# A decoder layer on one core: four key products of the context attention placed among the second projections, and rope's swap of halves done by copies on ACT

## The chip, the cores and the metric

The kernel runs on one core of a Trainium2 chip. The time is that of the device, in microseconds (us), for the whole program; the number that counts is the median of several runs. A profile of one execution stands beside it, taken by the hardware profiler.

The core's engines work side by side, each through its own queue and strictly in the order of that queue: PE (TensorE: matmuls), DVE (VectorE: elementwise work), ACT (ScalarE: activation functions, copies with a conversion), POOL (GpSimd: here, sums and maxima over the partitions) and SP (SyncE: here, it issues the DMAs). PE writes into PSUM, which is divided into eight banks; everything else lies in SBUF.

## The reference: what is computed

One decoder layer in fp32 on 8 batches of 100 tokens, D = 1024, with a context of 722 tokens for each batch:

```python
def _L0_xattn_ref(x, h_ctx_kv, ...):
    q = (x @ wq).reshape(B, L, NUM_HEADS, HEAD_DIM)          # 16 heads of 128
    k = (x @ wk).reshape(B, L, NUM_KV_HEADS, HEAD_DIM)       # 4 of 128
    v = (x @ wv).reshape(B, L, NUM_KV_HEADS, HEAD_DIM)
    q = rms_norm(q, q_norm_w)
    k = rms_norm(k, k_norm_w)
    k_ctx = (h_ctx_kv @ wk_ctx).reshape(B, T, NUM_KV_HEADS, HEAD_DIM)
    v_ctx = (h_ctx_kv @ wv_ctx).reshape(B, T, NUM_KV_HEADS, HEAD_DIM)
    k_ctx = rms_norm(k_ctx, k_norm_w)
    q = q * cos + rotate_half(q) * sin
    k = k * cos + rotate_half(k) * sin
    k_full = jnp.concatenate([k_ctx, k], axis=1)
    ...                                                       # causal softmax attention
    return out.reshape(B, L, NUM_HEADS * HEAD_DIM) @ wo

x = _layernorm(x + _L0_attn_ref(x, ...))      # retention, 8 heads
x = _layernorm(x + _L0_xattn_ref(x, context, ...))
x = _layernorm(x + _L0_ffn_ref(x, ...))       # silu(gate) * up, then down
```

The products that the change moves are `h_ctx_kv @ wk_ctx` for two of the four kv heads of batch 0. The swap of halves is `rotate_half`, in the queries and keys of the tokens (not of the context).

## The kernel before, in words

Every activation is kept transposed, features on the 128 partitions and tokens along the free axis. The 800 tokens are worked on in two halves of N = 400 (four batches each). So that fp32 accuracy comes out of the matmul's fp32r format, each operand is held as two parts, hi and lo: `split` makes hi by a cast on ACT (L69) and lo by a subtraction on DVE (L70). Each product is then three matmuls (`mm3`: L88 hi·hi, L89 hi·lo, L90 lo·hi), and a projection of 1024 features to 128 (`proj`) is 8 x 3 = 24 matmuls into one bank of PSUM. Banks come in three groups (L52): three of tag "a", four of "s", one of "v".

A weight comes in through `load_w`: a DMA of 512 KB into one of three buffers `wst`, then a split into one of four buffers `w`. The context weights were split earlier and lie in DRAM as `wcd`; `load_ws` brings one in as a DMA of 1 MB straight into a `w` buffer.

The stages follow each other: retention attention (l1), its output projection with LayerNorm (`out_proj`, half 0 and then half 1; its results are the split activations `z1`), the second projections (pool "l2"), the context attention (pool "cx"), the second output projection with LayerNorm, the feed-forward part. The order inside each engine's queue is not written out by hand: the framework's scheduler simulates the program with its own durations (L998) and orders each queue by that, so instructions of neighbouring stages are mixed at the seams. An order once fixed is kept by each engine.

Second projections, l2 (L570–594). For each of four kv heads there are four query heads (i = 0 to 3), one key (i = 4) and one value (i = 5), for both halves: 48 projections of `z1`, whose banks alternate between "a" and "s". A value is transposed, split and stored. Each of the 40 queries and keys goes through this:

- ACT squares the bank (L585), POOL sums the squares over the partitions (`all_red`, L127, into one of two buffers `ss`);
- `rope` (L130–140) multiplies the bank by the cosines (L136, whole) and by the sines with the halves of the partitions swapped (L137 and L138, 64 partitions each), all three on DVE reading PSUM, and adds the two results (L139, both in SBUF). After L138 the bank is free;
- `inv_root` (L112–123) makes the inverse root of the sum: Ln, Exp and Square on ACT (L115, L118, L120), two multiplies on DVE (L121 reads `ss` for the last time, L122);
- DVE multiplies the two (L590), `split2` divides the result into `d` (L69 on ACT, L70 on DVE), and SP stores it to DRAM (`qd`, `kd`).

Context attention, cx (L600 on). For each batch b, the context comes in through eight DMAs of 360 KB (`cs`, in the same three `wst` buffers; L609) and eight splits into four tiles `big`. Then for each kv head: two products for the keys (`proj(wk, ...)`, 362 and 360 columns), each followed by a square on ACT (L629), a sum over the partitions on POOL (L630), and the scaled keys as hi (ACT, L631) and lo (DVE, L632) in `kall`; two products for the values, which are transposed; scores; softmax; and the product with the values.

The tail of the LayerNorm of half 1 (`norm_late`, L298–309, and `scaled`, L264–269) stands right before the projections of half 1: a matmul gives the mean's last part (`delta`), ACT squares it (L304), DVE subtracts it from eight tiles `y` (L308) and from the variance (L305), `inv_root` follows, and for each of the eight tiles DVE scales `y` (L266), ACT casts it to hi and DVE subtracts for lo (L69, L70: these write `z`, that is `z1` of half 1).

Of the kernel before, what the change touches and what calls it, by code (L numbers as in the profile page):

```python
# [8 lines left out]
F32 = mybir.dt.float32  # L9
FR = mybir.dt.float32r  # L10
# [6 lines left out]
P = 128  # L17
# [24 lines left out]
def decoder_layer(ctx, tc, xT, cT, w1, wo1, w2, wo2, wc, w3, wd, gw, qw, kw, trig, dec, mask, out):  # L42
    nc = tc.nc

    def sbuf(name, bufs, side=None):
        return tc.tile_pool(name=name, bufs=bufs, side=side, reuse_waits="tile")
# [11 lines left out]
    def f32(ap):  # L58
        return ap.bitcast(F32)

    def bt(ap):
        return ap.rearrange("p (b t) -> p b t", b=NB)

    def split(dst, src):

        split2(dst[:, 0], dst[:, 1], src)
# [5 lines left out]
    def load_w(src, w=None, parts=1):  # L72
        st = wp.tile([P, KT * P], F32, tag="wst", name="wst", bufs=3)
        if w is None:
            w = wp.tile([P, 2, KT * P], FR, tag="w", name="w", bufs=4)
        for i in range(parts):
            c = slice(i * KT * P // parts, (i + 1) * KT * P // parts)
            nc.sync.dma_start(out=st[:, c], in_=src[:, c])
            split(w[:, :, c], st[:, c])
        return w  # L80

    def load_ws(i):
        w = wp.tile([P, 2, KT * P], FR, tag="w", name="w", bufs=4)
        nc.sync.dma_start(out=f32(w), in_=f32(wcd[i]))
        return w
# [16 lines left out]
    def proj(w, z, n=N, tag="a"):  # L102
        acc = bank(tag)[:, :n]
        for k in range(KT):
            t = z[k // QT]
            mmw(acc, w, k, t[:, 0, k % QT, :n], t[:, 1, k % QT, :n], k == 0, k == KT - 1)
        return acc
# [19 lines left out]
        nc.gpsimd.partition_all_reduce(y, x, P, op)  # L127
        return y

    def rope(pool, acc, cosw, sinw, tag="t1"):  # L130

        t1 = pool.tile([P, N], F32, tag=tag, name=tag)
        t2 = pool.tile([P, N], F32, tag="t2", name="t2")
        a = bt(acc)
        h = P // 2
        nc.vector.tensor_tensor(bt(t1), a, cosw[:, None, :].to_broadcast([P, NB, T]), ALU.mult)  # L136
        nc.vector.tensor_tensor(bt(t2[0:h]), a[h:P], sinw[h:P, None, :].to_broadcast([h, NB, T]), ALU.mult)  # L137
        nc.vector.tensor_tensor(bt(t2[h:P]), a[0:h], sinw[0:h, None, :].to_broadcast([h, NB, T]), ALU.mult)  # L138
        nc.vector.tensor_tensor(t1, t1, t2, ALU.add)  # L139
        return t1  # L140

    def tokens_first(pool, acc, copied=True):
# [23 lines left out]
    def big(shape):  # L166
        return bp.tile(shape, FR, tag="big", name="big")
# [29 lines left out]
    def load_constants(p, trg):  # L197
        dcy = p.tile([T, NH1, T], F32, name="dcy", bufs=1)
        nc.sync.dma_start(out=dcy, in_=dec)
        nc.sync.dma_start(out=msk, in_=mask)  # L200
        nc.sync.dma_start(out=wts[:, 0:2], in_=gw)
        nc.sync.dma_start(out=wts[:, 2:3], in_=qw)
        nc.sync.dma_start(out=wts[:, 3:4], in_=kw)

        nc.vector.tensor_scalar(gws, wts[:, 0:2], -8.0, None, ALU.mult)
        nc.vector.tensor_scalar(kws, wts[:, 3:4], -0.5 * math.sqrt(P), None, ALU.mult)
        nc.vector.tensor_scalar(tq, trg[:, 2:4], wts[:, 2:3], None, ALU.mult)
        nc.vector.tensor_scalar(tk, trg[:, 2:4], wts[:, 3:4], None, ALU.mult)
        return dcy


# [187 lines left out]
    with sbuf("l1", 2) as p:  # L399
# [37 lines left out]

        r4 = []

        def rope1(acc, cosw, sinw, tag):  # L440

            t1 = p.tile([P, N], F32, tag=tag, name=tag)
            t2 = p.tile([P, N], F32, tag="t2", name="t2")
            h = P // 2
            nc.scalar.copy(t2[0:h], acc[h:P])
            nc.scalar.copy(t2[h:P], acc[0:h])
            nc.vector.tensor_tensor(bt(t1), bt(acc), cosw[:, None, :].to_broadcast([P, NB, T]), ALU.mult)
            nc.vector.tensor_tensor(bt(t2), bt(t2), sinw[:, None, :].to_broadcast([P, NB, T]), ALU.mult)
            nc.vector.tensor_tensor(t1, t1, t2, ALU.subtract)
            return t1  # L450


        HB = ((0, 0), (1, 1), (0, 1), (1, 0))
        qk, v, oo, ss = {}, {}, {}, {}

        def of_qk(half, i, acc):
            qk[half, i] = rope1(acc, trg[:, 2 * i], trg[:, 2 * i + 1], f"qk{i}")

        def of_v(half, blk, acc, copied):
            tr = tokens_first(p, acc, copied)  # L460
# [106 lines left out]

    kapool = sbuf("ka", 2, "right")
    ka = kapool.__enter__()
    with sbuf("l2", 2) as p:  # L570
        for kv in range(NKV):
            for i0, i1 in ((0, 4), (4, 6)) if kv == 0 else ((0, 2), (2, 4), (4, 6)):
                ws = [load_w(w2[kv, i]) for i in range(i0, i1)]
                for half in range(2):
                    bs = slice(half * NB, (half + 1) * NB)
                    for i in range(i0, i1):
                        acc = proj(ws[i - i0], z1[half], tag=acc_tag())
                        if i == 5:
                            tr = tokens_first(p, acc).rearrange("p (b d) -> p b d", b=NB)
                            vs = p.tile([T, NB, 2, P], FR, tag="vs", name="vs", bufs=1)  # L580
                            split2(vs[:, :, 0], vs[:, :, 1], tr)
                            nc.sync.dma_start(out=f32(vd[kv, :, bs]), in_=f32(vs))
                            continue
                        sq = p.tile([P, N], F32, tag="sq", name="sq")
                        nc.scalar.activation(sq, acc, AF.Square)  # L585
                        ss = all_red(p, sq, "ss")
                        tb = tq if i < 4 else tk
                        t = rope(p, acc, tb[:, 0], tb[:, 1])
                        r = inv_root(p, ss, eps_k)
                        nc.vector.scalar_tensor_tensor(  # L590
                            t, t, -0.5 if i < 4 else -0.5 * math.sqrt(P), r, ALU.mult, ALU.mult)
                        d = p.tile([P, NB, 2, T], FR, tag="d", name="d", bufs=3)
                        split2(d[:, :, 0], d[:, :, 1], bt(t))
                        nc.sync.dma_start(out=f32(qd[kv, i, :, bs] if i < 4 else kd[kv, :, bs]), in_=f32(d))
# [4 lines left out]
    y2p = y2pool.__enter__()  # L599
    with sbuf("cx", 2) as p, sbuf("c1", 1) as p1:  # L600
        for b in range(B):
            cz = []
            for hf in range(2):
                n = SN[hf]
                z = [big([P, 2, QT, SH]) for _ in range(2)]
                for k in range(0, KT, 2):
                    cs = wp.tile([P, KT * P], F32, tag="wst", name="cs", bufs=3)
                    cs = cs[:, :2 * n].rearrange("p (k n) -> p k n", k=2)
                    nc.sync.dma_start(out=cs, in_=cT[b, :, k:k + 2, hf * SH:hf * SH + n])  # L609
                    split(z[k // QT][:, :, k % QT:k % QT + 2, :n], cs)  # L610
                cz.append(z)
            for kv in range(NKV):

                kall = ka.tile([P, 2, SC + T], FR, tag="kall", name="kall")
                nc.sync.dma_start(out=f32(kall[:, :, SC:]), in_=f32(kd[kv, :, b]))
                vall = p.tile([P, NC, 2, P], FR, tag="vall", name="vall")
                nc.sync.dma_start(out=f32(vall[C5:P, 5]), in_=f32(vd[kv, 0:P - C5, b]))
# [1 line left out]
                q = p.tile([P, 4, 2, T], FR, tag="q", name="q")  # L619
                nc.sync.dma_start(out=f32(q).rearrange("p h l t -> p h (l t)"),  # L620
                                  in_=f32(qd[kv, :, :, b]).rearrange("h p l t -> p h (l t)"))
                wk, wv = load_ws(2 * kv), load_ws(2 * kv + 1)
                sq = ka.tile([P, SC], F32, tag="ksq", name="ksq", bufs=1)
                ss = ka.tile([P, 6 * P], F32, tag="kss", name="kss", bufs=1)
                nc.gpsimd.memset(ss[:, SC:], 1.0)
                for hf in range(2):
                    n, at = SN[hf], slice(hf * SH, hf * SH + SN[hf])
                    acc = proj(wk, cz[hf], n)
                    nc.scalar.activation(sq[:, at], acc, AF.Square)  # L629
                    nc.gpsimd.partition_all_reduce(ss[:, at], sq[:, at], P, RED.add)  # L630
                    nc.scalar.activation(kall[:, 0, at], acc, AF.Copy, scale=kws)  # L631
                    nc.vector.scalar_tensor_tensor(kall[:, 1, at], acc, kws, f32(kall[:, 0, at]), ALU.mult, ALU.subtract)  # L632
                vt = p.tile([P, SC], F32, bufs=1, tag="cvt", name="cvt")
                for hf in range(2):
                    copy = nc.scalar.copy if hf == 0 else nc.vector.tensor_copy
                    copy(vt[:, hf * SH:hf * SH + SN[hf]], proj(wv, cz[hf], SN[hf]))
                for c0, c1, rows in ((0, 3, P), (3, 5, P), (5, 6, C5)):
                    tr = bank("s")
                    for c in range(c0, c1):
# [1 line left out]
                    src = tr[0:rows, 0:(c1 - c0) * P].rearrange("p (c d) -> p c d", d=P)  # L641
                    split2(vall[0:rows, c0:c1, 0], vall[0:rows, c0:c1, 1], src)

                row = dr.tile([6, P], F32, tag="row", name="row", bufs=2)
                nc.sync.dma_start(out=row.rearrange("c p -> (c p)")[None, :], in_=ss[0:1])
                rr = p.tile([P, 6], F32, tag="rr", name="rr")
                with nc.allow_non_contiguous_dma("a row turned into a column"):
                    nc.sync.dma_start(out=rr, in_=row.rearrange("c p -> p c"))
# [354 lines left out]
```

## Time and profile before

| what | value |
|---|---|
| runs, median (lowest to highest) | 2560.26 us (2559.32 to 2564.6) |
| profiled execution: own time | 2563.27 us |
| profiled execution: span | 2561.5 us |
| mean granted clock of PE | 0.993 |
| matmuls of l2 | from 572.4 to 829.9 us |
| rope in l2 on DVE | from 604.1 to 845.1 us |
| matmuls of one 128x400 product, start to start | 0.182 us |
| all-reduces, L127 writing `ss`: number, mean | 56, 2787 ns |

A busy time of an engine is the sum of its instructions' durations, where overlapping ones count once. "Idle before, releaser" is the time that an engine stood still ahead of an instruction, and the instruction that ended it. L-numbers are lines of the kernel before; a helper's line (L69, L70, L127) occurs in several stages, so its groups are told apart by the names of the tiles.

### The profile page before, as it was taken

What the parts mean: (1) busy time and instruction counts of PE and PEld (TensorE: products, weight loads), DVE (VectorE), ACT (ScalarE), POOL (GpSimd) and SP (SyncE); (2) the same over time, 40 slices, a digit from 0 to 9 for tenths busy, and PEclk for the clock granted to TensorE, in tenths of its full rate; (3) what the DMA queues carried; (4) which work ended last, traced back from release to release, by engine and by line L of the source; (5) the groups of instructions that cost most, each with busy time, mean ns of one, the idle gap of its engine ahead of it and who ended that gap; (6) DMA issues with size and microseconds to landing.
All of it is one profiled execution on the core that took longest, in us unless ns stands there. A gap on an engine that the chain in (4) does not pass through costs nothing.

```text
span 2561.5 us, 37457 instructions
## 1 busy us (share of the span) xinstructions
PE 2504.4 (98%) x14186; PEld 2464.7 (96%) x14186; DVE 2018.0 (79%) x3350; ACT 1294.3 (51%) x2310; POOL 468.8 (18%) x230
## 2 busy tenths in 40 slices
PE   8999999999988999999999999999999999999997
PEld 8999999998988999999999999999999999999996
DVE  6778876568999788898988988777865865865885
ACT  6676766335554455565656655444432432432451
POOL 0100011004444343433443443100000000000000
PEclk9999999999999999999999999999999999999999
DMA  7333445763335655454554455474411211211221
GB/s 236 108 125 120 147 142 207 247 227 114 135 131 181 200 176 165 144 177 147 160 174 152 154 183 176 149 259 131 153 50 66 83 50 65 84 50 65 68 74 52
DMA packets 165939, 353.91 MB, mean 138 GB/s; under 512 B 45531, under 2 KB 108379, under 8 KB 156543
## 3 DMA queue, kind: packets, MB, share of 16 engines
q1 hardware_dynamic: 164606, 347.33, 40.3%
q0 software_dynamic: 1152, 4.19, 1.0%
q8 instruction: 111, 1.82, 0.3%
q14 instruction: 70, 0.57, 0.1%
HBM read 283.09 MB, written 68.39 MB: 137 GB/s over the span
## 4 chain that ended last, share of the span: by engine, by line
PE 85%; DVE 9%; issue 2%; DMA 2%; ACT 1%; SPq 0%; DVEq 0%; ACTq 0%
PE a L88 16%; PE a L90 16%; PE a L89 16%; PE s L88 9%; PE s L89 9%; PE s L90 9%; PE v L88 3%; PE v L90 2%; PE v L89 2%; PE s L480 1%; DVE w L70 1%; DVE r L121 1%; DMA cs<-in_cT 1%; PE s L640 1%; DVE t L590 1%
## 5 line engine op out<-in xcount | busy, mean ns | idle before, releaser
L88 PE MATMUL a<-big,w 128*128 128x400 f32 (+2 forms) x1796 | 605.7, 338 | 7.3 <-ACT big L69 6.6
L89 PE MATMUL a<-big,w 128*128 128x400 f32 (+2 forms) x1796 | 605.2, 337 | 0.1
L90 PE MATMUL a<-big,w 128*128 128x400 f32 (+2 forms) x1796 | 603.8, 337 | 0.0
L69 ACT CAST w<-wst 128x1024 fp32r<-128x1024 f32 (+2 forms) x292 | 251.4, 864 | 271.2 <-PE a L90 120.0
L70 DVE TENSOR_TENSOR w<-wst,w 128x1024 fp32r<-128x1024 f32 (+2 forms) x292 | 294.2, 1010 | 107.3 <-ACT w L69 106.3
L88 PEld LDWEIGHTS a<-big,w 128*128 128x128 f32 x1796 | 338.2, 188 | 8.1 <-ACT big L69 6.6
L89 PEld LDWEIGHTS a<-big,w 128*128 128x128 f32 x1796 | 338.8, 189 | 1.6 <-DVE big L70 1.0
L90 PEld LDWEIGHTS a<-big,w 128*128 128x128 f32 x1796 | 339.0, 189 | 0.8 <-DVE w L70 0.2
L127 POOL PARTITION_ALL_REDUCE ss<-sq x56 | 155.6, 2787 | 358.3 <-DVE z L70 162.2
L88 PE MATMUL s<-big,w 128*128 128x400 f32 x596 | 207.9, 349 | 1.9 <-ACT big L69 1.9
L89 PE MATMUL s<-big,w 128*128 128x400 f32 x596 | 207.2, 348 | 2.0 <-DVE big L70 2.0
L90 PE MATMUL s<-big,w 128*128 128x400 f32 x596 | 206.4, 347 | 0.0
L630 POOL PARTITION_ALL_REDUCE kss<-ksq x64 | 167.9, 2624 | 142.2 <-ACT ksq L629 141.7
L69 ACT CAST w<-as 128x512 fp32r<-128x512 f32 x90 | 55.9, 621 | 213.2 <-PE a L90 180.8
L676 ACT ACTIVATE s<-s,rk 128x400 f32<-128x400 f32 x160 | 88.1, 591 | 93.7 <-DVE sm L698 60.6
L827 DVE TENSOR_TENSOR s<-s 128x400 f32<-128x400 f32 x183 | 102.7, 571 | 25.1 <-ACT s L823 19.3
L127 POOL PARTITION_ALL_REDUCE mb<-sm x32 | 83.3, 2602 | 200.9 <-DVE sm L698 200.9
L88 PEld LDWEIGHTS s<-big,w 128*128 128x128 f32 x596 | 112.7, 189 | 4.0 <-ACT big L69 3.1
L695 ACT ACTIVATE s<-s 128x800 f32<-128x800 f32 (+1 forms) x128 | 95.0, 749 | 42.2 <-DVE s L689 39.3
L89 PEld LDWEIGHTS s<-big,w 128*128 128x128 f32 x596 | 112.7, 189 | 3.4 <-DVE big L70 2.5
L90 PEld LDWEIGHTS s<-big,w 128*128 128x128 f32 x596 | 113.3, 190 | 0.0
L70 DVE TENSOR_TENSOR pl<-s,ph 128x800 fp32r<-128x800 f32 (+1 forms) x128 | 108.4, 851 | 2.1 <-ACT ph L69 1.5
(311 smaller groups left out, 6196.2 us busy)
## 6 DMA issues: line engine op xcount, KB each, us to landing
wst<-in_w SPq DMA_DIRECT2D x137, 512.0 KB
w<-wcd SPq DMA_DIRECT2D x64, 1024.0 KB
wst<-in_wo SPq DMA_DIRECT2D x64, 512.0 KB
wst<-in_wd SPq DMA_DIRECT2D x32, 512.0 KB
big<-o1d SPq DMA_DIRECT2D x16, 800.0 KB
qd<-d SPq DMA_DIRECT2D x32, 400.0 KB
q<-qd SPq DMA_DIRECT2D x32, 400.0 KB
o2d<-oh SPq DMA_DIRECT2D x32, 400.0 KB
```

The source lines that it names most:

```text
L69: nc.scalar.copy(hi, src)
L70: nc.vector.tensor_tensor(lo, src, f32(hi), ALU.subtract)
L88: nc.tensor.matmul(acc, lh, rh, start=start, stop=False, skip_group_check=chain)
L89: nc.tensor.matmul(acc, lh, rl, start=False, stop=False, skip_group_check=chain)
L90: nc.tensor.matmul(acc, ll, rh, start=False, stop=stop, skip_group_check=chain)
L121: nc.vector.scalar_tensor_tensor(q, ss, eps, q, ALU.add, ALU.mult)
L127: nc.gpsimd.partition_all_reduce(y, x, P, op)
L480: nc.tensor.matmul(bt(o)[:, b], vv[:, b * P:(b + 1) * P], pf[:, b], start=True, stop=True)
L630: nc.gpsimd.partition_all_reduce(ss[:, at], sq[:, at], P, RED.add)
L676: nc.scalar.activation(sc, sp, AF.Copy, scale=rk[:, c:c + 1])
L695: nc.scalar.activation(e, e, AF.Exp)
L827: nc.vector.tensor_tensor(t, x, y, op)
```

## The change

Three things are altered.

1. `rope` takes the form that the retention stage had under the name `rope1`: ACT copies the two halves of the bank, swapped, into `t2`; DVE multiplies the bank by the cosines and `t2` by the sines (this one reads SBUF alone), and adds. The two halves of the sine tables of queries and keys (`tq`, `tk`) are swapped once at the start, by six small copies. `rope1` is gone, and the retention stage calls `rope` with a subtraction.
2. The loads and splits of a batch's context become a function, `load_context`. That of batch 0 is called within l2, before the weights of kv 0's key and value (i0 = 4); in the order that the scheduler makes of it, its eight DMAs follow those of the weights of the first four projections on SP, and its splits stand among the tail of the LayerNorm of half 1. The other batches' are where they were.
3. The keys of the context become `context_keys`, with a `step` for each of the two parts. For batch 0, the keys of kv 0 and kv 1 are made within l2, one part ahead of each of four groups of projections. Their `kall` and their row of sums are kept in the list `early` until the context attention takes them. The values' `cvt` moves to the pool "ka".

```diff
-    def rope(pool, acc, cosw, sinw, tag="t1"):
+    def rope(pool, acc, cosw, sinw, tag="t1", op=ALU.add):
         t1 = pool.tile([P, N], F32, tag=tag, name=tag)
         t2 = pool.tile([P, N], F32, tag="t2", name="t2")
-        a = bt(acc)
         h = P // 2
-        nc.vector.tensor_tensor(bt(t1), a, cosw[:, None, :].to_broadcast([P, NB, T]), ALU.mult)
-        nc.vector.tensor_tensor(bt(t2[0:h]), a[h:P], sinw[h:P, None, :].to_broadcast([h, NB, T]), ALU.mult)
-        nc.vector.tensor_tensor(bt(t2[h:P]), a[0:h], sinw[0:h, None, :].to_broadcast([h, NB, T]), ALU.mult)
-        nc.vector.tensor_tensor(t1, t1, t2, ALU.add)
+        nc.scalar.copy(t2[0:h], acc[h:P])
+        nc.scalar.copy(t2[h:P], acc[0:h])
+        nc.vector.tensor_tensor(bt(t1), bt(acc), cosw[:, None, :].to_broadcast([P, NB, T]), ALU.mult)
+        nc.vector.tensor_tensor(bt(t2), bt(t2), sinw[:, None, :].to_broadcast([P, NB, T]), ALU.mult)
+        nc.vector.tensor_tensor(t1, t1, t2, op)
...
+        for t in (tq, tk):
+            sw = p.tile([P, T], F32, tag="vt", name="sw", bufs=1)
+            nc.vector.tensor_copy(sw, t[:, 1])
+            nc.vector.tensor_copy(t[0:P // 2, 1], sw[P // 2:P])
+            nc.vector.tensor_copy(t[P // 2:P, 1], sw[0:P // 2])
...
+    def load_context(b):
+        cz.clear()
+        for hf in range(2):
+            n = SN[hf]
+            z = [big([P, 2, QT, SH]) for _ in range(2)]
+            for k in range(0, KT, 2):
+                cs = wp.tile([P, KT * P], F32, tag="wst", name="cs", bufs=3)
+                cs = cs[:, :2 * n].rearrange("p (k n) -> p k n", k=2)
+                nc.sync.dma_start(out=cs, in_=cT[b, :, k:k + 2, hf * SH:hf * SH + n])
+                split(z[k // QT][:, :, k % QT:k % QT + 2, :n], cs)
+            cz.append(z)
+
+    def context_keys(kv):
+        kall = ka.tile([P, 2, SC + T], FR, tag="kall", name="kall")
+        wk = load_ws(2 * kv)
+        sq = ka.tile([P, SC], F32, tag="ksq", name="ksq", bufs=1)
+        ss = ka.tile([P, 6 * P], F32, tag="kss", name="kss", bufs=1)
+        row = dr.tile([6, P], F32, tag="row", name="row", bufs=2)
+        nc.gpsimd.memset(ss[:, SC:], 1.0)
+        def step(hf):
+            n, at = SN[hf], slice(hf * SH, hf * SH + SN[hf])
+            acc = proj(wk, cz[hf], n)
+            nc.scalar.activation(sq[:, at], acc, AF.Square)
+            nc.gpsimd.partition_all_reduce(ss[:, at], sq[:, at], P, RED.add)
+            nc.scalar.activation(kall[:, 0, at], acc, AF.Copy, scale=kws)
+            nc.vector.scalar_tensor_tensor(kall[:, 1, at], acc, kws, f32(kall[:, 0, at]), ALU.mult, ALU.subtract)
+            if hf:
+                nc.sync.dma_start(out=row.rearrange("c p -> (c p)")[None, :], in_=ss[0:1])
+        return step, (kall, row)
...
     with sbuf("l2", 2) as p:
         for kv in range(NKV):
             for i0, i1 in ((0, 4), (4, 6)) if kv == 0 else ((0, 2), (2, 4), (4, 6)):
+                if (kv, i0) == (0, 4):
+                    load_context(0)
                 ws = [load_w(w2[kv, i]) for i in range(i0, i1)]
+                if (kv, i0) in ((1, 2), (2, 2)):
+                    step, kept = context_keys(kv - 1)
+                    early.append(kept)
+                if (kv, i0) in ((1, 2), (2, 0), (2, 2), (3, 0)):
+                    step(i0 == 0)
...
-            cz = []
...
+            if b > 0:
+                load_context(b)
             for kv in range(NKV):
-
-                kall = ka.tile([P, 2, SC + T], FR, tag="kall", name="kall")
+                if early:
+                    kall, row = early.pop(0)
+                else:
+                    step, (kall, row) = context_keys(kv)
+                    step(0)
+                    step(1)
```

More of the change, by code (lines that the diff above doesn't have):

```diff
@@ L438, in decoder_layer @@
         r4 = []
[L440 to L450, printed above, removed]
         HB = ((0, 0), (1, 1), (0, 1), (1, 0))
@@ L456, in of_qk @@
         def of_qk(half, i, acc):
-            qk[half, i] = rope1(acc, trg[:, 2 * i], trg[:, 2 * i + 1], f"qk{i}")
+            qk[half, i] = rope(p, acc, trg[:, 2 * i], trg[:, 2 * i + 1], f"qk{i}", ALU.subtract)
         def of_v(half, blk, acc, copied):
@@ L569, in decoder_layer, with context_values @@
     ka = kapool.__enter__()
+    cz = []
+    def load_context(b):
[26 more added lines that the diff above has]
+        return step, (kall, row)
+    def context_values(kv):
+        wv = load_ws(2 * kv + 1)
+        vt = ka.tile([P, SC], F32, bufs=1, tag="cvt", name="cvt")
+        for hf in range(2):
+            copy = nc.scalar.copy if hf == 0 else nc.vector.tensor_copy
+            copy(vt[:, hf * SH:hf * SH + SN[hf]], proj(wv, cz[hf], SN[hf]))
+        return vt
+    early = []
     with sbuf("l2", 2) as p:
@@ L601, in decoder_layer @@
         for b in range(B):
-            cz = []
[L603 to L611, printed above, removed]
-            for kv in range(NKV):
-                kall = ka.tile([P, 2, SC + T], FR, tag="kall", name="kall")
+            if b > 0:
+                load_context(b)
+            for kv in range(NKV):
+                if early:
[4 more added lines that the diff above has]
+                    step(1)
                 nc.sync.dma_start(out=f32(kall[:, :, SC:]), in_=f32(kd[kv, :, b]))
@@ L621, in decoder_layer @@
                                   in_=f32(qd[kv, :, :, b]).rearrange("h p l t -> p h (l t)"))
[L622 to L636, printed above, removed]
+                vt = context_values(kv)
                 for c0, c1, rows in ((0, 3, P), (3, 5, P), (5, 6, C5)):
@@ L642, in decoder_layer @@
                     split2(vall[0:rows, c0:c1, 0], vall[0:rows, c0:c1, 1], src)
-                row = dr.tile([6, P], F32, tag="row", name="row", bufs=2)
-                nc.sync.dma_start(out=row.rearrange("c p -> (c p)")[None, :], in_=ss[0:1])
                 rr = p.tile([P, 6], F32, tag="rr", name="rr")
```

## The prediction, made before the changed kernel had run

> **What bounds the kernel now.** I read the page first: what is busy, and the chain that ended last.
>
> ```profile
> PE 2504.4 (98%) x14186; PEld 2464.7 (96%) x14186; DVE 2018.0 (79%) x3350; ACT 1294.3 (51%) x2310; POOL 468.8 (18%) x230
> ...
> PE 85%; DVE 9%; issue 2%; DMA 2%; ACT 1%; SPq 0%; DVEq 0%; ACTq 0%
> ```
>
> TensorE is busy 2504.4 of 2561.5 us: whatever the change brings has to come out of 57 us of idle time, and of slow clock. Where is that? The windows by 50 us (stretch; then busy time of PE, PEld, DVE, ACT, POOL with the instructions; granted clock, DMA share, GB/s):
>
> ```profile
> 600.00:650.00 50.00, 44.55 (x239) 43.81 (x238) 47.99 (x79) 29.93 (x57) 30.09 (x10) 0.97 0.39 134
> 650.00:700.00 50.00, 47.02 (x261) 46.66 (x260) 49.30 (x76) 25.66 (x50) 24.07 (x9) 1.00 0.37 130
> 700.00:750.00 50.00, 46.23 (x256) 45.84 (x254) 49.26 (x72) 26.84 (x50) 20.83 (x9) 0.99 0.37 128
> 750.00:800.00 50.00, 45.30 (x240) 45.18 (x241) 48.79 (x68) 25.03 (x47) 21.24 (x8) 0.90 0.43 142
> 800.00:850.00 50.00, 39.89 (x208) 39.16 (x207) 46.03 (x76) 24.01 (x49) 21.61 (x9) 0.90 0.69 245
> 850.00:900.00 50.00, 50.00 (x303) 49.29 (x302) 37.45 (x69) 25.12 (x52) 15.67 (x10) 1.00 0.52 169
> ```
>
> From 600 to 850, the second projections (pool l2), PE lacks 5.45+2.98+3.77+4.70+10.11 = 27.0 us while DVE is 97% busy; from 850 on, in the context attention, PE lacks nothing. The waits of PE say who is late, the end of rope, which frees the accumulator's bank:
>
> ```profile
> PE a L88 <- DVE t L138: 25.7, 5, 8.5
> ```
>
> After four of these five gaps the matmuls start 0.333 us apart instead of 0.182; I count some 50 such, 50 x 0.15 = 7.3 us more. So l2 loses about 34 us, and its bound is DVE. Its last rope-related work there ends at 846.
>
> Why does DVE need 242 us for 40 ropes? The timeline of DVE, then of POOL, then of PE:
>
> ```profile
> 618.94 1.23 DVE L70 TENSOR_TENSOR w<-wst,w 128x1024 fp32r<-128x1024 f32 x1
> ...
> 621.06 0.62 DVE L121 SCALAR_TENSOR_TENSOR r<-ss,eps_k,r 128x400 f32<-128x400 f32 x1
> ...
> 622.09 2.76 DVE L70 TENSOR_TENSOR w<-wst,w 128x1024 fp32r<-128x1024 f32 x1
> ```
>
> ```profile
> 621.78 2.86 POOL L127 PARTITION_ALL_REDUCE ss<-sq  x1 [1.83 <-DVE r L121]
> ```
>
> ```profile
> 628.65 0.42 PE L88 MATMUL a<-z,w 128*128 128x400 f32 x1 [4.16 <-DVE t L138]
> ```
>
> The same weight split takes 2.76 us instead of 1.23 when it starts just after an all-reduce. These start right behind L121, which frees their output; the DVE operation starting some 0.3 us later loses 1.5 us if both its inputs lie in SBUF. The PSUM-reading multiplies of rope never do (next fence). Summing start-to-start intervals over l2, the stalls come to 34.6 us, 22 to 23 of them.
>
> **What the Trainium skill says.** "SBUF — State Buffer", section "Who interferes with whom": a DVE instruction with two SBUF inputs contends with a GpSimd instruction that reads SBUF, one with at most one SBUF input doesn't, and ACT never waits. The trace agrees: 2.76 against 1.23 us, and L138 from 567 to 569 ns in all 40 uses. "TensorE: Matmul & The Clock Gate", section "What's actually happening": an idle window of about 3.4 us takes PE to half clock. The trace has 0.333 against 0.182 us after gaps of 4.16 to 8.48 us.
>
> **The change part by part.**
>
> ```profile
> L138 DVE TENSOR_TENSOR t<-s,tq x16: 567/568/569, 605.2 to 826.3; 64x400 f32<-64x400 f32 x16
> ...
> L139 DVE TENSOR_TENSOR t<-t,t x40: 559/569/2177, 607.6 to 845.1; 128x400 f32<-128x400 f32 x40
> ...
> L445 ACT COPY t<-a x11: 488/490/492, 14.7 to 408.3; 64x400 f32<-64x400 f32 x11
> ...
> L448 DVE TENSOR_TENSOR t<-t,trg x32: 565/570/584, 16.2 to 412.3; 128x400 f32<-128x400 f32 x32
> ```
>
> These rows (ns, minimum, median, maximum) hold the old rope and, in L445 and L448, the new one, which the retention stage already uses.
>
> 1. Rope. Removed: L137 and L138, which start every 0.589 and 0.598 us, 1.187 together. Added on DVE: one multiply of two SBUF tiles; such 128x400 operations start every 0.486. So -0.70 x 40 = -28.1 us of DVE. Added on ACT: 40 x (0.490+0.485) = 39 us. ACT has 131.7 busy in these 250 us, so there is room. But DVE now waits for ACT's queue, where the copies stand behind casts of 1 us. In the retention stage DVE never idled ahead of L448; here it has no slack. I put 5 us, between 0 and 15.
>
> 2. The stalls. L139 and the new multiply are both open to the lock, and the shield (three PSUM multiplies in a row) shrinks to one. In the instruction order before, 26 of 40 L121 are followed by PSUM multiplies at the first or second place. In the new order 26 of 40 are followed by none in the first three places (or by one only in the third: 20 + 6), 13 have one at once and then a two-SBUF operation, one has two. At 1.5 us for the 26, 1.15 for the 13 (the 0.58-us multiply covers part of the lock), 0.6 for the one and 1.3 for each of the four all-reduces of the keys: 39 + 15 + 0.6 + 5.2 = 60 us against 34.6: +25. From below: 0, if the starts fall otherwise; from above: all 44 at 1.5 us, 66, so +31.
>
> 3. The context of batch 0. Its eight loads and splits leave l2 (-8 x 0.98 = -7.8 us of DVE there; L609 issued them from 773 to 812). They now stand on SP behind the first weights of l2, and their splits on ACT and DVE stand in the norm's tail of out_proj, ahead of z1 of half 1. The tail before:
>
> ```profile
> 588.75 3.94 DVE L308 TENSOR_TENSOR y<-y,s 128x400 f32<-128x400 f32 x8 [2.42 <-ACT vs L304]
> ...
> 600.17 3.98 DVE L70 TENSOR_TENSOR z<-y,z 128x400 fp32r<-128x400 f32 x8
> ```
>
> Three wst buffers carry these loads, each released by its lo split, so they go in a chain. With 4 us from issue to cast: first issue 574.75, fourth context cast at 590.2; the ACT square of L304, which stands behind it on ACT, at 591.0 (588.2 before); L308 from 591.8; last context cast 601.5; L121 602.65 (595.0); z's lo from 607.9 to 611.9. So z1 is 7.7 us late: PE, which starts half 1 at 602.5, waits from then to 608.4, some 6 us plus 1.8 of slow clock, and DVE's l2 starts 7.8 us late. How long do such loads take?
>
> ```profile
> 773.56 4.26 DMA cs<-in_cT
> ...
> 916.40 6.62 DMA cs<-in_cT
> ```
>
> At 4 us the delay is the 7.7; at 7 us, by the same chain, about 17.
>
> 4. The keys. For kv 0 and 1, 96 matmuls of 362 or 360 columns (0.166 us apart: 15.8 us) go to l2's queue of PE, where they can fill the 27 us of gaps, and leave the stretch after 846 that has no gap. That is where the gain is. Their DVE part, four kall splits of about 0.5, two of which stood in this stretch before: +1.5 with waits. Their four ACT squares, four copies and two weight loads of 1 MB were issued soon after anyway; SP has no queue that binds here.
>
> 5. Six tiny copies in load_constants: under 1 us at a time when DVE waits; nothing.
>
> Sum for DVE: +7.8 - 28.1 + 25 - 7.8 + 1.5 + 5 = +3.4, so l2's end goes from 846 to 849.4. PE stands there as far ahead of DVE as before, but with 15.8 us of keys behind it: the end of the kernel moves by 3.4 - 15.8 = -12.4 us. PE after that point has no gap to lose it in. On the profiled execution's own time, 2563.3, that is 2550.9; its span goes from 2561.5 to 2549. The runs' median lies 3.0 under the profiled execution, so 2548.
>
> **The rivals.**
>
> A, the stalls don't grow: PE becomes the bound in l2. Without +25, DVE would end long before PE. Then PE's l2 loses only the late start (7.5 of the 34.3): -26.8, or 2533.5 at the very best; with small waits left, 2537. For it: PE's work with keys is 5.75 us per rope, DVE's about 5.7 after the change, so small shifts decide. Against: L139's maximum of 2177 ns; the lock is seen and more operations are open to it.
>
> B, no measurable change: the loads take 7 us in the tail. Then z1 is 17 us late, 9 more than in my sum, and 2548 becomes 2557. For it: 6.62 at 916; against: 4.26 at 773, in l2 itself.
>
> C, slower: the ACT queue becomes rope's bound. The new multiply waits for a copy that stands behind a 1-us cast or behind an Ln (L115) that waits for an all-reduce, and so PE's banks, DVE and POOL run in one ring. It decides from (12.4 + 5.1) / 40 = 0.44 us of DVE idle per rope beyond the 0.13 that I have counted; at 0.6 us it gives 2572. For it: DVE has only 7.3 us of idle time in l2 before, no slack to catch up. Against: in the new order the Ln of one rope stands behind the copies of the next, and ACT is under 75% busy.
>
> D, the keys don't fill the gaps: their products need an "a" bank and a slot of w (four buffers), and the projections behind them wait for both. Then PE's gaps stay, 15.8 us are only moved, and the rest of the sum (+3.4) gives 2564, at the edge of what can be told.
>
> **How the numbers follow.** The measurement can tell 0.2%, 5.1 us: faster is under 2555.1, slower over 2565.4. My forecast (2540 to 2554): 0.52; A (2533 to 2540): 0.14; B and the nearer half of D (2555 to 2565): 0.19; C and the rest of D: 0.15. Faster 0.66, same 0.19, slower 0.15. Predicted 2548; the range reaches from A's 2535 to 2564.
>
> **What would show it.** In the profile after: PE's loss from 600 to 850 falls from 27 us to about 10 to 15, most of it one gap near 602; L138's waits turn to the new full multiply of the accumulator and shrink; rope's full multiply from PSUM stays at 0.57, while the SBUF multiply and L139 show many at 2.1; z's lo splits begin near 608; DVE stays over 95% busy until about 849. I would be wrong if DVE idles in l2 ahead of the SBUF multiply (C), if z1 comes after 615 (B), if DVE's l2 ends before 835 (A), or if the waits of PE name the weights or a bank of the keys (D).

## The result, and the profile after

The changed kernel takes 2550.86 us (median of 6 runs, 2549.36 to 2552.38), the kernel before 2561.11 in the same runs (six of them; the 2560.26 in the table above is the median of three): ratio 0.9958, 95% interval 0.9945 to 0.9971. It is 10.2 us faster; 12.4 were forecast (2548, range 2535 to 2564). The profiled execution has a span of 2550.0 us.

The page after, the same two lines:

```profile
PE 2504.3 (98%) x14186; PEld 2462.7 (97%) x14186; DVE 2006.9 (79%) x3316; ACT 1338.8 (53%) x2390; POOL 471.7 (18%) x230
...
PE 87%; DVE 7%; DMA 2%; issue 2%; ACT 1%; SPq 0%; DVEq 0%; ACTq 0%
```

PE works as long as before (2504.3 against 2504.4), DVE 11 us less and ACT 45 more. The gain is idle time of PE that is gone. The windows by 50 us (busy time of PE, PEld, DVE, ACT, POOL; granted clock, DMA share, GB/s) say where:

```profile
600.00:650.00 50.00, 42.98 (x218) 42.01 (x217) 48.54 (x71) 36.94 (x72) 26.57 (x9) 0.93 0.43 149
650.00:700.00 50.00, 45.17 (x251) 44.36 (x249) 48.44 (x69) 33.20 (x66) 29.60 (x10) 1.00 0.43 146
700.00:750.00 50.00, 48.65 (x258) 47.72 (x259) 45.47 (x66) 36.30 (x70) 25.29 (x11) 0.93 0.49 159
750.00:800.00 50.00, 49.08 (x275) 48.70 (x274) 46.77 (x64) 35.62 (x68) 27.96 (x12) 1.00 0.40 134
800.00:850.00 50.00, 48.51 (x273) 47.59 (x273) 41.66 (x63) 31.32 (x63) 20.77 (x8) 1.00 0.56 193
```

From 600 to 700 us PE does 3.4 us less than before (88.15 against 91.57); in the next 150 us it does 14.8 more (146.24 against 131.42), and there DVE is no longer full. Together 11.4, which is the change of the span. The waits of PE over the whole program, from the longest down (two shorter ones left out at the dots):

```profile
PE a L88 <- ACT big L69: 6.4, 1, 6.4
PE a L88 <- ACT w L69: 5.4, 3, 3.1
PE a L88 <- ACT r L120: 4.3, 1, 4.3
PE s L150 <- ACT vt L147: 3.0, 4, 0.9
...
PE a L88 <- DMA w<-wcd: 2.2, 1, 2.2
```

The 25.7 us behind rope have gone; the first line was there before (6.6), in another stage. The 4.3 us are still rope's: the matmul at 634.88 needs the bank that the cosine multiply frees at 634.74, although the profile names the ACT instruction that ended nearest. The rows of the sine multiply and of the addition (ns: minimum, median, maximum):

```profile
L138 DVE TENSOR_TENSOR t<-t,tq x32: 557/564/2164, 611.2 to 826.7; 128x400 f32<-128x400 f32 x32
...
L139 DVE TENSOR_TENSOR t<-t,t x40: 557/563/2176, 612.8 to 842.0; 128x400 f32<-128x400 f32 x40
```

Both are now caught by the lock, the wait of a DVE instruction with two SBUF inputs for POOL's reads: 2164 and 2176 ns. To size it, I take each DVE interval from start to start, from the first rope of l2 to the last, and add up what lies over the median of its kind ("excess" below). It was 33.6 us before and is 53.2 after (the prediction had 34.6 for the same trace of before, so the figure is good to about 1 us). One such pair, POOL's timeline and then DVE's:

```profile
618.97 2.98 POOL L127 PARTITION_ALL_REDUCE ss<-sq  x1 [3.08 <-DVE r L121]
```

```profile
619.45 2.06 DVE L138 TENSOR_TENSOR t<-t,tq 128x400 f32<-128x400 f32 x1
```

The tail of the norm, DVE's timeline, and the context loads in the chain of that stretch:

```profile
591.95 3.93 DVE L313 TENSOR_TENSOR y<-y,s 128x400 f32<-128x400 f32 x8
...
606.81 3.97 DVE L70 TENSOR_TENSOR z<-y,z 128x400 fp32r<-128x400 f32 x8
```

```profile
582.37 3.07 DMA cs<-in_cT
587.23 3.03 DMA cs<-in_cT
596.72 3.05 DMA cs<-in_cT
```

The lo parts of z start at 606.81 (600.17 before). In this execution l2's first matmul starts 2.25 us later than in the one shown of before, so counted from there the delay is 4.4 us, not 7.7. (The table above has l2's matmuls from 572.4 to 829.9 us; that is wrong. In that trace they run from 573.5 to 834.2, and the counts below use these.) The loads landed in about 3.05 us where I had put 4.

### The profile page after: what moved, and what is told of

It is laid out like the page before. It is cut to its first block, busy times and chain, and to the rows that moved or that the text cites. A ratio compares the mean times of both kernels' runs of the same rounds, so it can differ in the third digit from the quotient of the medians.

```text
span 2550.0 us, 37518 instructions
## 1 busy us (share of the span) xinstructions
PE 2504.3 (98%) x14186; PEld 2462.7 (97%) x14186; DVE 2006.9 (79%) x3316; ACT 1338.8 (53%) x2390; POOL 471.7 (18%) x230
## 4 chain that ended last, share of the span: by engine, by line
PE 87%; DVE 7%; DMA 2%; issue 2%; ACT 1%; SPq 0%; DVEq 0%; ACTq 0%
PE a L90 16%; PE a L88 16%; PE a L89 16%; PE s L89 10%; PE s L90 10%; PE s L88 10%; PE v L88 3%; PE v L90 2%; PE v L89 2%; DVE r L122 1%; PE s L473 1%; PE s L668 1%; DVE r L121 1%; DVE d L70 1%; DVE w L70 1%
## 5 line engine op out<-in xcount | busy, mean ns | idle before, releaser
L69 ACT CAST w<-wst 128x1024 fp32r<-128x1024 f32 (+2 forms) x292 | 251.4, 864 | 260.4 <-PE a L90 112.0
L127 POOL PARTITION_ALL_REDUCE ss<-sq x56 | 161.2, 2885 | 332.7 <-DMA zd<-y 166.6
L69 ACT CAST w<-as 128x512 fp32r<-128x512 f32 x90 | 55.9, 621 | 214.2 <-PE a L90 180.1
```

Source lines behind the costliest of these rows:

```text
L69: nc.scalar.copy(hi, src)
```

## The experiments

All times are medians. Twelve kernels ran, in three groups of four, and the kernel before took 2561.4 to 2561.6 in each group; they are told here by question. Code that is left out of an edit is marked by dots.

### Which part makes the gain

**The rope alone**: the kernel before with the new rope and the swapped sine tables, nothing else.

```diff
-        nc.vector.tensor_tensor(bt(t1), a, cosw[...], ALU.mult)
-        nc.vector.tensor_tensor(bt(t2[0:h]), a[h:P], sinw[h:P, ...], ALU.mult)
-        nc.vector.tensor_tensor(bt(t2[h:P]), a[0:h], sinw[0:h, ...], ALU.mult)
+        nc.scalar.copy(t2[0:h], acc[h:P])
+        nc.scalar.copy(t2[h:P], acc[0:h])
+        nc.vector.tensor_tensor(bt(t1), bt(acc), cosw[...], ALU.mult)
+        nc.vector.tensor_tensor(bt(t2), bt(t2), sinw[...], ALU.mult)
...
```

> The kernel before with the new rope alone (copies on ACT, sine tables swapped at the start); context and keys where they were. Theory 1 (the keys make the gain, rope's saving on DVE goes into stalls behind POOL): DVE loses 28 to 32 us of rope work in l2 and gains some 20 us of stalls and some 5 us of waiting for ACT, so l2 ends 3 to 7 us earlier: 2554 to 2558. Theory 2 (the rope makes the gain, the keys add little): 2548 to 2552. If this kernel's l2 starts some 2 us later than before, the small copies at the start cost it.

Measured 2561.26, ratio 1.0 (0.9992 to 1.0008): nothing. Theory 2 falls, and theory 1 was some 3 us too hopeful.

**The early context and keys alone**: the changed kernel with the old rope in l2 and the sine tables as they were. The retention stage keeps its copies on ACT.

```diff
-        nc.scalar.copy(t2[0:h], acc[h:P])
-        nc.scalar.copy(t2[h:P], acc[0:h])
...
+        nc.vector.tensor_tensor(bt(t2[0:h]), a[h:P], sinw[h:P, ...], ALU.mult)
+        nc.vector.tensor_tensor(bt(t2[h:P]), a[0:h], sinw[0:h, ...], ALU.mult)
...
```

> The changed kernel with the old rope in l2 (three multiplies from PSUM) and without the swapped tables: the early context and the four key products alone. Theory 1: PE fills its gaps with 15.8 us of keys; DVE starts l2 4 us late, has no context splits there (-7.8), four kall splits (+2.2) and stalls from four more all-reduces (+5): net +3 to +5, so 2548 to 2551. Theory 2: DVE was the bound and gets no relief, so no gain: 2558 to 2564. l2 starts at 572 to 573 if the copies at the start cost something.

Measured 2558.23, ratio 0.9986 (0.9980 to 0.9993): 3.2 us faster. That is at the lower end of theory 2's range; its "no gain" is not quite so, and theory 1 falls.

**The rope and the early context, without the early keys.**

```diff
-                if (kv, i0) in ((1, 2), (2, 2)):
-                    step, kept = context_keys(kv - 1)
-                    early.append(kept)
-                if (kv, i0) in ((1, 2), (2, 0), (2, 2), (3, 0)):
-                    step(i0 == 0)
```

> The changed kernel without the early keys: the new rope and the early context alone, all keys in the context attention. If the keys make what the rope alone (2561.3) doesn't: 2557 to 2560, the load giving DVE 7.8 - 4.4 = 3.4 us at most. If it is the context splits that leave l2: 2551 to 2554.

Measured 2563.94, ratio 1.0010 (1.0002 to 1.0018): 2.5 us slower than before, and outside both expectations. So the early keys, put on top of these two, are worth 13.1 us of their 15.8; with the old rope, the same keys and load together are worth 3.2. The early context alone with the old rope was not run, so how much of those 3.2 us its late z takes away is not known.

Why the parts don't add up can be read by counting each profile from the first matmul of l2:

| kernel | first rope | last rope's multiply ends | PE's last projection ends | keys in it | DVE: excess, idle |
|---|---|---|---|---|---|
| before | +30.6 | +268.3 | +260.7 | 0 | 33.6, 7.3 |
| rope alone | +30.5 | +261.4 | +258.9 | 0 | 53.1, 11.8 |
| context and keys alone | +35.1 | +272.9 | +270.6 | 15.8 | 33.3, 11.0 |
| rope and context | +35.2 | +263.8 | +261.7 | 0 | 52.2, 15.3 |
| all (the changed kernel) | +34.9 | +265.6 | +263.2 | 15.8 | 53.2, 12.3 |

DVE's end moves nearly as a sum: the rope -7, the rest +4.6, all -2.7. PE's end, less the keys, moves by -1.8, -5.9, +0.9 and -13.3. It stood 7.6 us ahead of DVE before and stands 2.2 to 2.4 ahead in all the others of the table: 5 us are lost once, to whichever part comes first, and that is where the sum of the parts differs from the whole. It is a count, not yet a cause. These positions are of one execution each and scatter by a microsecond or two.

Where PE stands instead, with the rope alone, its waits from 574 to 850 us show:

```profile
PE s L150 <- ACT vt L147: 15.0, 3, 6.9
PE a L88 <- DVE t L137: 9.0, 2, 7.3
```

L150 transposes the values and stands in PE's queue in order; L147 is ACT's copy ahead of it. In the case of 6.9 us, ACT's timeline has that copy behind three waits for DVE, the last of them at a rope copy:

```profile
760.01 0.63 ACT L115 ACTIVATE r<-ss,eps_k 128x400 f32<-128x400 f32 x1 [1.76 <-DVE r L122]
761.46 0.53 ACT L69 CAST d<-t 128x400 fp32r<-128x400 f32 x1 [0.82 <-DVE t L595]
763.49 0.49 ACT L135 COPY t<-s 64x400 f32<-64x400 f32 x1 [1.50 <-DVE t L139]
...
764.94 0.47 ACT L147 COPY vt<-a 128x400 f32<-128x400 f32 x1
```

L135 waits for L139, which frees t2, and L139 took 2.11 us there, behind an all-reduce. The rope and context alone show 16.7 us behind L147; the changed kernel 3.0, before 1.3. This is the ring of rival C, in a place that I had not named. That this wait ate the rope's gain is read from the trace; no run here takes the wait away. Nor does it need rope's copies: the context and keys alone, which have none in l2, show 8.7 us behind L147.

**Three buffers t2** loosen that link, in the rope alone and in the changed kernel.

```diff
-        t2 = pool.tile([P, N], F32, tag="t2", name="t2")
+        t2 = pool.tile([P, N], F32, tag="t2", name="t2", bufs=bufs)
...
-                        t = rope(p, acc, tb[:, 0], tb[:, 1])
+                        t = rope(p, acc, tb[:, 0], tb[:, 1], bufs=3)
```

> The rope alone (the kernel before with the copies) with three buffers t2. With two, DVE's work in l2 fell by 11 us and the time not at all, while PE waited 15.0 us for ACT's copies of the values (1.3 before), one of them 6.9 us behind a copy for which t2 was not free. Theory 3 (that ring ate rope's gain): the 15 us fall to 2 to 6, 2551 to 2556. Rival (the wait is only where the loss shows): 2559 to 2562.

> The changed kernel with three buffers t2 in place of two. Copies on ACT stood 8.1 us behind L139, which frees t2. Theory 3 (ACT's in-order queue behind t2 costs PE time): 2546 to 2549. Rival: no change, 2550 to 2552.

Measured 2563.75 (1.0012, 1.0005 to 1.0018) and 2555.14 (0.9974, 0.9965 to 0.9984): both slower than with two buffers, by 2.5 and 4.3 us, where neither expectation had them. In the rope alone the edit did what it was for: from 574 to 850 us ACT waits 3.1 us for L139, in place of 18.4. But its casts of `d` (L69) now wait 48.8 us for the DVE multiply ahead of them, in place of 22.0, and PE still waits 14.0 us for L147. Theory 3 falls in that form: t2 is one link of ACT's in-order queue behind DVE, and with that link loosened the queue waits at the next. With a third buffer the scheduler also orders the queues anew, so these two runs change more than the buffer.

### What paces DVE: the lock

**A tenth of POOL's sums**, in the changed kernel and in the kernel before. Nine tenths of the sums are left out; what reads them reads the same forty columns ten times, so the work of the other engines keeps its size.

```diff
-                        ss = all_red(p, sq, "ss")
+                        ss = p.tile([P, 40], F32, tag="ss", name="ss")
+                        nc.gpsimd.partition_all_reduce(ss, sq[:, 0:40], P, RED.add)
+                        ss = ss[:, None, :].to_broadcast([P, 10, 40])
...
```

> The changed kernel, where POOL's sum over the partitions in l2 takes 40 of the 400 columns, and what reads it reads these 40 ten times over (nine tenths of the sums are left out). Theory 1 (the stalls behind POOL are what DVE loses after the change, 53 us over the plain intervals): they fall under 12 us, DVE has slack throughout l2, and PE's losses there (16 us of gaps, 5 of slow clock) fall by 8 to 14: 2537 to 2543. Rival (the ring of ACT's queue and the t2 buffers holds PE, whatever POOL does): 2547 to 2551.

> The same cut of the sums in the kernel before. Its stalls were 34 us. Theory 1: DVE needs some 25 us less for l2, and of PE's 28 us of gaps and 7 of slow clock 20 to 27 vanish: 2534 to 2541. Rival (the gaps come from the order of the queues): 2550 to 2558. If both e6 and e7 follow theory 1, the whole of the change's gain was also to be had from the stalls.

Measured 2532.62 (0.9887, 0.9874 to 0.9901) and 2532.16 (0.9885, 0.9871 to 0.9898): 18.2 us under the changed kernel, 29.4 under the kernel before, and the same time. The rivals fall, and both gains are larger than theory 1 had them. The windows of the changed kernel with the short sums:

```profile
600.00:650.00 50.00, 47.05 (x261) 46.33 (x260) 46.41 (x84) 44.07 (x86) 11.65 (x10) 1.00 0.54 185
650.00:700.00 50.00, 50.00 (x280) 49.94 (x279) 44.28 (x82) 38.31 (x77) 12.67 (x10) 1.00 0.49 169
700.00:750.00 50.00, 50.00 (x283) 49.96 (x282) 39.91 (x66) 39.39 (x74) 11.46 (x12) 1.00 0.45 151
```

PE has no gap left from 650 to 750 us. And in the kernel before with the short sums, the addition:

```profile
L139 DVE TENSOR_TENSOR t<-t,t x40: 560/569/585, 608.6 to 818.9; 128x400 f32<-128x400 f32 x40
```

Its maximum is 585 ns, where it was 2177; the excess falls from 33.6 to 3.6 us (and from 53.2 to 12.3 in the other). So without the stalls the change as a whole is worth nothing (its parts were not run that way): what it gains, it gains only where stalls hold DVE up. The short sum is also sooner done (a median of 0.71 us in the changed kernel and 0.76 in the kernel before), and these two runs don't part its latency from the lock; the next two do. In the kernel before, the 30.0 us of excess that vanish are as much as the whole gain of 29.4.

**The sums on PE**, in the changed kernel and in the kernel before. One matmul with a tile of ones into bank v, which is free in l2. The squares are rounded to fp32r before they are summed; that is a change in the computation.

```diff
+        oner = p.tile([P, P], FR, tag="oner", name="oner", bufs=1)
+        nc.scalar.activation(oner, onem, AF.Copy, scale=float(D))
...
-                        sq = p.tile([P, N], F32, tag="sq", name="sq")
+                        sq = p.tile([P, N], FR, tag="sq", name="sq")
                         nc.scalar.activation(sq, acc, AF.Square)
-                        ss = all_red(p, sq, "ss")
+                        sv = bank("v")[:, :N]
+                        nc.tensor.matmul(sv, oner, sq, start=True, stop=True)
+                        ss = p.tile([P, N], F32, tag="ss", name="ss")
+                        nc.scalar.copy(ss, sv)
```

> The changed kernel, where PE instead of POOL sums the 40 squares of l2 over the partitions (one matmul of the squares, in fp32r, with a tile of ones, into the free bank v; ACT copies the sums out). Theory 1: the stalls are gone as with the short sums (2532.6), and 40 matmuls of 0.182 us are added, 7.3: 2538 to 2543. Rival: the single bank v makes PE wait for ACT's copy, 2545 to 2555.

> The same replacement in the kernel before. Theory 1: 2532.2 with the short sums, plus 7.3: 2538 to 2542, the same as e14 within 3 us, since with no lock DVE has no need of the rope's or the keys' relief. Rival: 2545 to 2555.

Measured 2541.14 (0.9919, 0.9905 to 0.9932) and 2540.73 (0.9917, 0.9904 to 0.9931). Theory 1 holds: 2532.2 + 7.3 = 2539.5 for the second. Both are some 10 us faster than the changed kernel, the second by seven new lines in the kernel before. Its windows:

```profile
650.00:700.00 50.00, 50.00 (x280) 49.90 (x279) 48.95 (x87) 34.23 (x66) 0.00 (x0) 1.00 0.43 151
700.00:750.00 50.00, 50.00 (x278) 49.95 (x277) 47.47 (x83) 33.92 (x64) 0.00 (x0) 1.00 0.48 156
750.00:800.00 50.00, 50.00 (x279) 49.86 (x279) 48.15 (x82) 36.13 (x68) 0.00 (x0) 1.00 0.69 219
```

DVE is nearly as full as before (47.5 to 49.0 of 50 us, where it was 48.8 to 49.3), but with 82 to 87 instructions per window in place of 68 to 76, and PE has no gap: busy was not the same as late.

These two runs also part the lock from the latency. From the end of a square to its finished sums the median is 7.2 us in the kernel before and 8.3 with the sums on PE; in the changed kernel it is 3.7 and 6.5. The sums come later than POOL's did, and the time still falls. What is gone is the stretching of DVE: the excess in the second of these kernels is about 3 us.

### Where the pieces stand

**The context loaded one group later.**

```diff
-                if (kv, i0) == (0, 4):
+                if (kv, i0) == (1, 0):
                     load_context(0)
```

> The changed kernel with the context of batch 0 loaded one group later (before the projections 0 and 1 of kv 1). Theory 1: half 1 of z1 comes 3 to 4 us earlier, and five or more of the eight context splits go back into l2 on DVE (+5 to +7): within 4 us of the changed kernel, 2549 to 2555. Rival: the late z1 is what costs, 2545 to 2547.

Measured 2560.38, ratio 0.9997 (0.9989 to 1.0005): 9.5 us lost, more than either expectation had. z was not sooner to any use: its lo parts started at 604.89, but one split stood among them and one behind them, so that the first rope came 37.3 us after l2's start (34.9 in the changed kernel), and the four other splits went between the first ropes. There PE waits for a bank:

```profile
PE a L88 <- DVE t L137: 13.3, 2, 10.8
```

The last rope ends at +273.3 instead of +265.6, 7.7 us later: the first rope came 2.4 later, and the four splits behind it took 5.2 us on DVE, one of them stretched to 2.45.

**The keys one to three groups earlier.**

```diff
-                if (kv, i0) in ((1, 2), (2, 2)):
-                    step, kept = context_keys(kv - 1)
+                if (kv, i0) in ((1, 0), (1, 4)):
+                    step, kept = context_keys(len(early))
                     early.append(kept)
-                if (kv, i0) in ((1, 2), (2, 0), (2, 2), (3, 0)):
-                    step(i0 == 0)
+                if (kv, i0) in ((1, 0), (1, 2), (1, 4), (2, 0)):
+                    step((kv, i0) in ((1, 2), (2, 0)))
```

> The changed kernel with the four key products one to three groups earlier (ahead of kv 1's three groups and kv 2's first). Most of what PE still loses in l2 after the change lies before 700 us (12 of 15 us, and some 4 us at slow clock). Theory 1: the keys now fill two of these gaps, 4 to 8 us less: 2543 to 2547. Rival: the gaps are DVE's, and only move, 2549 to 2552.

Measured 2554.87, ratio 0.9972 (0.9962 to 0.9983): 4.0 us slower than the changed kernel; neither expectation. The gap near 54 us after l2's start is still there (5.6 us), 4.4 us go to the keys' weights (L84), and late gaps come back, one of 4.8 us at 257. The gap near 54 could not be filled this way: the matmul that ends it is a projection's, and the first key product stands behind it in PE's queue, at +82.

**The values' copies first on ACT.**

```diff
-            nc.scalar.copy(vt, acc)
+            with tc.high_priority():
+                nc.scalar.copy(vt, acc)
```

> The changed kernel with high priority for ACT's copies of the values, ahead of the transposes for which PE waited 3.0 us in the changed kernel (7.7 and 6.3 in the slower variants with earlier keys and with three buffers t2). If the place of these copies in ACT's queue is what sets the variants apart: 2547 to 2550. If the order of all queues together does, and the changed kernel's happens to be a good one: 2552 to 2558.

Measured 2552.09, ratio 0.9963 (0.9950 to 0.9977): 1.2 us over the changed kernel, which their intervals don't tell apart. PE waits 3.3 us for these copies, as before the edit (3.0), so the edit did not do what it was for, and the question is not answered. What sets the variants with earlier keys and with three t2 apart from the changed kernel, some 4 us at the same work, stays open: DVE's excess is the same in all (53 to 55 us), its idle time is 15.4 and 16.6 instead of 12.3.

## Why the prediction was right

**The place of the gain, and its size.** Keys into l2's gaps, out of a stretch that has none: shown by the kernel without early keys (13.1 us slower). The sum gave -12.4; measured -10.2. That it came so near is in part luck, for within it errors cancelled:

- *Rope.* Forecast -28.1 us of DVE, with 0.70 per rope. The cosine multiply's interval to the next instruction fell too, from 0.578 to 0.484 us, which was not in the sum, so it is 0.795 per rope, -31.8.
- *Stalls.* Forecast from 34.6 to 60, +25; measured from 33.6 to 53.2, +19.6. The count by instruction order was of the right kind, a quarter too high. They fall on more rows than L138 and L139: of the 53.2, L122 has 14.5, L138 13.9 and L636 (L590 before) 9.9. That the stalls are POOL's was argued from overlap then, and is shown by the short sums and by the sums on PE.
- *ACT.* Forecast 5 us of idle time on DVE, behind rope's copies; measured 5.0 in all (7.3 to 12.3). The copies account for 7.0 us, but 5.6 of them stand ahead of the cosine multiply and only 1.4 ahead of the sine multiply, where I had expected them; idle slivers of under 0.06 us, most of them between the PSUM multiplies, fell from 2.8 to 0.8. So the equal number is luck. ACT's queue also holds PE directly, at the values' transposes. That was not in the sum; in the rope alone PE waits 15.0 us there.
- *The late z.* Forecast 7.7 us, measured 4.4, since loads took 3.05 us; I had put 4 from 4.26 at a busier time. PE lost 2.0 us there, not 6.
- *DVE's end.* Forecast +3.4, measured -2.7 (counted from l2's start): 6 us too pessimistic, above all from rope, stalls and the late z.
- *The lead.* "PE stands there as far ahead of DVE as before" was wrong. The lead fell from 7.6 to 2.4 us, 5.2 lost. The two errors cancel to -13.3 at PE's last projection.
- *Small slips.* 50 x 0.15 is 7.5 us of slow clock, not 7.3, and ACT's busy time in the five windows adds up to 131.5, not 131.7. Neither moves the sum.
- *The rest.* -13.3 there, -11.5 in the span, -10.2 in the medians. The profiled execution of before is one in which l2 began at 573.5; in all twelve kernels here, with the small copies at the start or without, it begins at 574.5 to 576.2. So that part looks like scatter between executions (before has one profiled execution only), and not like a cost of part 5.

**The signs named beforehand.** PE's loss from 600 to 850 fell from 27.0 to 15.6 us, just over the 10 to 15 named; but most of it was not near 602. DVE did not stay over 95% until 849: it falls to 91, 94 and 83% from 700 on. The second half of l2 is bound by PE, and the first half by DVE still: the balance of rival A was reached by half.

**The rivals.** A, as an account of this change, is out: the stalls grew. Its number for an l2 in which PE is hardly held up, 2533.5, is near what the changed kernel took with the short sums, 2532.6; but there the stalls were gone, where A only had them not grow, so the nearness is in part luck. Nor does its "DVE would end long before PE" come out of the prediction's own sums: without the +25, DVE ends at 824.4, and PE's last projection at 834.2 - 26.8 + 15.8 = 823.2. B did not occur; the loads were shorter, not longer. C occurred in part: in the rope alone PE waits 15.0 us behind ACT's queue and nothing is gained, in the changed kernel it waits 3.0; that the wait is the cause is argued, not shown. D is out for the kernel as it is (gaps were filled); with the old rope the outcome is nearer to it: there the keys, with the early context, brought 3.2 us of 15.8.

**The lock and the clock.** The Trainium skill, "SBUF — State Buffer", section "Who interferes with whom", gave the rule on which the largest uncertain term stood: a DVE instruction with two SBUF inputs contends with GpSimd's reads, one with a PSUM input doesn't. The runs agree: excess 33.6 us with POOL's full sums, 3.6 with a tenth of them, and L138 of the old rope, reading PSUM, never over 571 ns in any of them. It names no price; here it was 1.5 us for a 0.57-us operation. "TensorE: Matmul & The Clock Gate", section "What's actually happening", puts half clock behind an idle window of about 3.4 us. The traces agree in part. In l2 of all fourteen kernels, every gap of PE from 3.11 us up has a stretch at half clock beside it. But shorter gaps can have one too: in the changed kernel those of 4.32, 3.11 and 2.00 us have it, that of 2.17 us has not. So 3.4 us is no sharp limit for a gap here. With the short sums, where only a gap of 2.36 us is left, the clock stays at 1.00.

## What to carry to other kernels

Ask of a full engine whether its instructions are long or stretched: compare maximum and median of one row, and look at what ran beside the maximum. Here 34 us of "busy" DVE were waits behind POOL, and moving POOL's sums to PE, for 7.3 us of matmuls, gained 20.7 us where the change gained 10.2. An edit that swaps PSUM inputs for SBUF inputs saves instructions and opens more of them to such a lock; work moved into gaps fills only those that it stands ahead of in the engine's queue, as the earlier keys showed at the gap near 54 us.

## What had not been expected

- The cosine multiply from PSUM starts the next instruction after 0.578 us before and 0.484 after; its own duration is 0.56 to 0.57 in both. Before, a multiply of 64 partitions follows it. That the follower reads PSUM is not the reason: in the changed kernel a split that reads PSUM follows once, and in the rope alone another cosine multiply, both after 0.484. The multiplies of 64 partitions start the next one after 0.589 to 0.607, whether that reads PSUM or SBUF. Why stays open.
- A stretched operation of 128x400 mostly ends 2.2 to 2.5 us after POOL's start, ahead of the end of POOL's 2.6 to 3.0 us as the profile has it (its spans on POOL are rough): the sine multiply of 619.45 ends at 621.51, the all-reduce at 621.95.
- The same work in another order: four kernels with all the parts of the change (the changed one, three t2, earlier keys, values first) lie between 2550.9 and 2555.1.
- A context load took 3.05 us in the norm's tail, 4.26 within l2 and 6.62 in the context attention: the same 360 KB.
